# Two graph attention layers on sparse edges: three row tiles put first, their edges from five late tiles gathered apart, and light and heavy tiles interleaved

## The chip, the cores and the metric

The kernel runs on one core of one Trainium2 chip, in one launch, without help from the host. The metric is the device time in microseconds of a whole execution, as a median over several runs.

## The reference

There are 4096 nodes with 512 features and an adjacency matrix of 4096 x 4096 integers. An edge from node i to node j is likelier the smaller both numbers are, so the first row tiles have many edges and the last few. Two blocks follow one another, each with the old value added and a layer norm:

```
def attention(x, adj, W, a):                # for each head
    h = x @ W                               # 4096 x 64, eight heads (or x 512, one head)
    e = leaky_relu(src(h)[:, None] + dst(h)[None, :], 0.2)
    e = where(adj > 0, e, very_negative)
    return softmax(e, axis=-1) @ h

x = layernorm(x + attention(x, adj, W, a))              # block 0: 8 heads of 64
h = elu(attention(x, adj, W1, a1))                      # block 1: 8 heads of 64
h = elu(attention(h, adj, Wo, ao))                      #          1 head of 512
y = relu(h @ lin1_w + lin1_b) @ lin2_w + lin2_b         #          512 -> 1024 -> 512
x = layernorm(x + y)
```

A node without any edge gets the mean of all h, which is what the softmax over equal scores gives.

## The kernel before, in words

The kernel works on edges, not on the full matrix. Nodes stand in 32 row tiles of 128. There are four stages.

**Edge search** (find_edges). For each row tile, its part of the adjacency is loaded (raw), turned into signs by ScalarE (sg), and TensorE builds a key for each column (key); VectorE takes the largest eight of each segment and sorts them out into a list (cand, lst). ScalarE and GpSimd then find where each row's edges begin and end in one long list for the tile (degs, counts, starts, ends, sides), TensorE lays the list out (pl), and the result is idx: chunks of 128 edges each, one edge a partition, whose value is the number of the column's node. nl says to which row the edge belongs. A `Part` is such a list over a range of columns; tile 0 has four, every other tile one. There are 35 parts and 309 chunks: tile 0 has 51 chunks, tile 1 has 21, tiles 5 and 6 have 11, tiles 7, 9 and 10 have 10, 9 and 9, tiles 31 to 29 have 5. Beside it, the projection for layer 0 is made (`beside`).

**Layer 0 and layer 1** (heads_layer, called twice), and the **tail** with layer 2 and the two dense layers. Each layer has a table in DRAM with one row of projected values for each node and one more, row N, with their mean. A tile's chunks are cut into units of at most six chunks. For each unit:

- `gather` takes a buffer g and issues one indirect DMA on GpSimd's queue for each chunk, which brings 128 table rows;
- `spread` brings the rows' own scores to the edges with small matmuls (pss), once a tile;
- `weights` adds the gathered scores (z) and takes the exponent on ScalarE;
- `add` builds a selection matrix (sm), scales the gathered rows (g, line 1200; in layer 2 the weight goes into sm, line 1187), and TensorE accumulates them by row into acc (line 1212).

After a tile's last unit its sum is divided, normed and projected for the next layer's table: divide, norm, project, rows and split are steps that `run` takes one at a time between the units of the following tiles, so that a tile's row is written some units after its last accumulation. `rows` calls project_out, whose DMA on the SP queue writes 128 rows of the next table (line 711); `split` prepares the scores of eight tiles. Row N needs all tiles: mean_of_all_but makes it from all but the last tile ahead of the last unit, and finish_mean adds the last and writes it (line 770). In the layers the order of the tiles is 31 down to 0, in the tail it is written out by hand in `blocks` of two or four tiles, because the dense layers (first_dense, second_dense; 16 matmuls of 512 columns to a piece) work on a block at a time. Their pieces are spread over the units of the next block by `pace` and `due`.

Which instruction stands where on each engine's queue follows from this program order, since these stages run under a manual schedule; DMA issues on SP can be moved by the framework when what they wait for is ready earlier. Buffers set how far gathers run ahead:

```
g buffers in layers 0 and 1:  GB = 7, gather(units[i + GB]) stands right after add(units[i])
g buffers in the tail:        GT = 4, another pool, opened when the layers' pools are closed
order in each iteration:      weights(units[i + 1]); add(units[i]); gather(...); the ways of earlier tiles
```

In layer 0 ScalarE clears the seven buffers first (line 1286), in the tail GpSimd clears the four (line 1424). The tail then loads the weights of the dense layers on SP (lines 1428 to 1434) and turns the first bias with a transpose on TensorE (line 1503).

Of the kernel before, what the change touches and what calls it, by code (L numbers as in the profile page):

```python
# [10 lines left out]
F32 = mybir.dt.float32  # L11
# [29 lines left out]
GC = 6  # L41
GB = 7
KW = 512
FAR = -1e30
WIDE = 21
GT = 4

# [23 lines left out]
class Part:  # L71
# [5 lines left out]
    def __init__(self, t, lo, hi, last):  # L77
        self.t, self.lo, self.hi, self.last = t, lo, hi, last
        top = t * P
        r = 3 if t == 0 else 1  # L80
        self.segs = []
        j = lo
        while j < hi:
            lim = min(hi, (j // 1024 + 1) * 1024)
            lam, k = 0.0, j
            while k < lim:
                more = lam + rate(top, k)
                if k - j >= 8 * r and tail(more, 8 * r) > 3e-7:
# [20 lines left out]
        assert self.off > 0 and self.chunks[0] + self.chunks[1] >= self.n  # L109

# [448 lines left out]
def sparse_path(  # L559
# [291 lines left out]
    def find_edges(big, sb, ps, pk, constants, sg, beside):  # L851
# [12 lines left out]
        for v, p in enumerate(pts):  # L864
            t, k, c0, nch = p.t, p.k, p.first, p.n
            if t > 0:
                sg = signs_of(sb, t)
# [151 lines left out]
    def blocks_in(p, lo, m):  # L1019


        out = []
        for i in range(p.blocks):
            mine = [(g, c - lo) for g, c in enumerate((i, p.off + i)) if i < p.chunks[g] and lo <= c < lo + m]
            if len(mine) == 2:
                out.append((i, slice(0, 2), slice(mine[0][1], mine[1][1] + 1, p.off)))
            elif mine:
                g, c = mine[0]
                out.append((i, slice(g, g + 1), slice(c, c + 1)))
        return out  # L1030

    class Unit:

        def __init__(self, t, runs, slots):
            self.t, self.runs, self.slots = t, runs, slots
            self.chunks = [c for first, n in runs for c in range(first, first + n)]
# [10 lines left out]
    def units_of(order):  # L1049
        units = []  # L1050
        for t in order:
            own = [
                Unit(t, [(p.first + i, n) for i, n in runs], slots)
                for p in pts if p.t == t for runs, *slots in p.units()
            ]
# [9 lines left out]
    class Attention:  # L1065
# [6 lines left out]
        def gather(self, u):  # L1072

            u.g = self.gp.tile([P, GC, F + HS], F32, name="g")
            for k, c in enumerate(u.chunks):
                nc.gpsimd.indirect_dma_start(  # L1076
                    out=u.g[:, k, : self.st.row],
                    out_offset=None,
                    in_=self.st.table[:, :],
                    in_offset=bass.IndirectOffsetOnAxis(ap=idx[:, c : c + 1], axis=0),  # L1080
                    bounds_check=N,
                    oob_is_err=False,
# [187 lines left out]
    def heads_layer(gp, wk, sb, pp, st, nxt, fetch, finish, clear):  # L1270

        order = list(range(NT - 1, -1, -1))
        units = units_of(order)
        with tc.tile_pool(name=f"ha_{st.name}", bufs=2, space=PSUM, reuse_waits="tile") as pacc, \
# [5 lines left out]
            if clear:  # L1283
                for _ in range(GB):
                    g = gp.tile([P, GC * (F + HS)], F32, name="g")
                    nc.scalar.activation(g, ones.to_broadcast(g.shape), AF.Copy, scale=0.0)
            for u in units[:GB]:
                at.gather(u)
            for t in order[:2]:
# [23 lines left out]
            def split(t):  # L1313
                split_s(pp, nxt, t, 8)

# [7 lines left out]

            ways = []
            for i, u in enumerate(units):
# [16 lines left out]
                if u.first and pos > 0:  # L1342
                    ways.append((divide, order[pos - 1]))
                    run(divide)
                if spread:
                    spread()
            ways.append((divide, order[-1]))
            while ways:
# [57 lines left out]
    layers.close()  # L1406
    with tc.tile_pool(name="tg", bufs=GT, side="right", reuse_waits="tile") as gp, \
            tc.tile_pool(name="tb", bufs=1, side="right", reuse_waits="tile") as big, \
# [5 lines left out]
        few = NT - 12  # L1414
        blocks = [[NT - 1, NT - 2], [NT - 3 - i for i in range(NJ)]]
        blocks += [[1 + b, few // 2 - b, few // 2 + 1 + b, few - b] for b in range(few // NJ)]
        blocks.insert(3, [NT - 9, 0, NT - 8, NT - 7])
        blocks.append([NT - 10, NT - 11])
# [3 lines left out]
        at = Attention(st2, gp, wk, pacc, ps)  # L1422
        for _ in range(GT):
            nc.gpsimd.memset(gp.tile([P, GC, F + HS], F32, name="g"), 0.0)
        for u in units[:GT]:
            at.gather(u)
        l1w = big.tile([P, FC, HID], F32, name="sl1w")
# [84 lines left out]
        for i, u in enumerate(units):  # L1512
# [9 lines left out]
            at.add(u)  # L1522
            if i + GT < len(units):
                at.gather(units[i + GT])
            close()
# [71 lines left out]
```

## Time and profile before

| | us |
|---|---|
| median of 3 runs | 2143.87 (2143.78 to 2149.99) |
| the profiled execution | 2328.89 |
| its span, first to last instruction | 2326.7 |
| edge search | 0 to 497 |
| layer 0 (first gather to first gather) | 500 to 1032 |
| layer 1 | 1032 to 1556 |
| tail | 1556 to 2327 |

| engine | busy us | share of the span |
|---|---|---|
| PE (TensorE matmul) | 1776.6 | 76% |
| DVE (VectorE) | 1328.1 | 57% |
| POOL (GpSimd) | 1161.8 | 50% |
| ACT (ScalarE) | 658.9 | 28% |

In the page, PEld is TensorE's loading of weights, SP the queue of the direct DMAs, and L1212 is line 1212 of the kernel. A line of a timeline has the start, the duration, the engine, the line, the operation, what it writes and reads, the number of instructions merged, and in brackets the idle time before it with what ended it. The busy time of POOL counts a gather's descriptor work, not the transfer. The granted TensorE clock was 0.885 of full speed on average.

### The profile page before, as it was taken

How to read it: one execution, taken by the hardware profiler on the slowest of the kernel's cores; microseconds unless marked ns; L12 is line 12 of the kernel's file. 1: busy time of each engine (PE TensorE's matmuls, PEld its weight loads, DVE VectorE, ACT ScalarE, POOL GpSimd, SP SyncE). 2: the span in 40 equal slices, each digit the busy share in tenths (PEclk: the TensorE clock that was granted, in tenths of full speed). 3: DMA queues.
4: the chain of work that ended last, by engine and by line, in shares of the span. 5: the costliest groups of instructions: out<-in, count | busy, mean ns of one | idle time of the engine just before them, and what ended most of it. 6: DMA issues, size and time to landing. Idle time of an engine off the chain costs nothing.

```text
span 2326.7 us, 29282 instructions
## 1 busy us (share of the span) xinstructions
PE 1776.6 (76%) x8987; PEld 1038.4 (45%) x8987; DVE 1328.1 (57%) x3920; ACT 658.9 (28%) x2311; POOL 1161.8 (50%) x1662
## 2 busy tenths in 40 slices
PE   4778776643987775754997767746999898998997
PEld 3555442212665543531665444424445444444444
DVE  6887776744998776733777655733243424334322
ACT  3446776650332211100433221101111111121121
POOL 5424444456556664627556665646355634444300
PEclk9989997866999896875999988877999999999999
DMA  6434665525667775625566665545354524335301
GB/s 222 141 115 159 224 256 207 210 80 163 201 209 219 212 209 144 174 60 145 154 159 170 175 182 145 158 128 143 87 150 131 170 81 148 101 110 151 93 16 52
DMA packets 132589, 351.94 MB, mean 151 GB/s; under 512 B 41922, under 2 KB 42954, under 8 KB 128454
## 3 DMA queue, kind: packets, MB, share of 16 engines
q0 software_dynamic: 74160, 206.25, 33.1%
q1 hardware_dynamic: 58262, 143.72, 17.5%
q8 instruction: 74, 1.21, 0.2%
q14 instruction: 93, 0.76, 0.1%
HBM read 347.31 MB, written 42.24 MB: 167 GB/s over the span
## 4 chain that ended last, share of the span: by engine, by line
PE 36%; DVE 12%; issue 9%; another core or an unknown queue 6%; DMA 3%; POOL 3%; ACT 2%; SPq 0%; DVEq 0%; POOLq 0%; ACTq 0%
PE acc L1212 13%; PE p L1475 9%; PE ph L697 6%; PE p L1487 5%; DVE g L1200 4%; POOL g L1076 3%; DMA g<-table_t,idx 2%; DMA xr<-sx_d 1%; PE pt L683 1%; DVE bs L1253 1%; DVE sm L1179 1%; DVE sm L1187 1%; DVE xr L1492 1%; DVE z L1147 1%
## 5 line engine op out<-in xcount | busy, mean ns | idle before, releaser
L1076 POOL DMA_INDIRECT g<-table_t,idx x927 | 937.4, 1011 | 720.1 <-PE acc L1212 352.9
L1212 PE MATMUL acc<-g,sm 128*64 128x260 f32 (+2 forms) x4068 | 619.9, 424 | 219.9 <-DVE g L1200 100.7
L1212 PEld LDWEIGHTS acc<-g,sm 128*64 128x64 f32 x4068 | 347.9, 150 | 462.7 <-issue 177.8
L697 PE MATMUL ph<-sw_t,xt 128*128 128x264 f32 (+1 forms) x1536 | 408.4, 415 | 82.1 <-ACT xt L686 46.3
L697 PEld LDWEIGHTS ph<-sw_t,xt 128*128 128x128 f32 x1536 | 303.4, 204 | 154.2 <-ACT xt L686 63.0
L1200 DVE TENSOR_TENSOR g<-g,wp 128x2048 f32<-128x2048 f32 (+3 forms) x132 | 349.1, 2645 | 22.8 <-ACT wp L1155 20.2
L884 DVE MAX8 cand<-key 128x8 f32<-128x353 f32 (+55 forms) x467 | 197.3, 449 | 77.7 <-PE key L878 77.1
L1475 PE MATMUL p<-sht,sl1w 128*128 128x512 f32 (+1 forms) x576 | 229.3, 553 | 2.2 <-issue 1.2
L1487 PE MATMUL p<-sl2w,shid 128*128 128x512 f32 x512 | 227.0, 598 | 0.0
L686 ACT ACTIVATE xt<-pt 128x128 f32<-128x128 f32 x384 | 101.1, 278 | 286.5 <-PE pt L683 132.3
L710 ACT COPY hrow<-ph 128x260 f32<-128x260 f32 (+2 forms) x194 | 71.1, 373 | 311.1 <-PE ph L697 146.2
L1475 PEld LDWEIGHTS p<-sht,sl1w 128*128 128x128 f32 x576 | 107.6, 191 | 114.0 <-issue 108.7
L1487 PEld LDWEIGHTS p<-sl2w,shid 128*128 128x128 f32 x512 | 95.4, 190 | 120.1 <-issue 119.3
L1249 DVE SCALAR_TENSOR_TENSOR o<-ex,o 128x512 f32<-128x512 f32 x64 | 44.4, 694 | 182.8 <-ACT ex L1248 145.1
L877 PE MATMUL key<-sg,s_identb 128*128 128x512 bf16 (+1 forms) x258 | 111.6, 434 | 15.4 <-DVE cand L884 10.1
L848 ACT ACTIVATE sg<-raw 128x4096 bf16<-128x4096 int32 (+1 forms) x39 | 116.9, 2998 | 6.6 <-DMA raw<-in_adj_dram 3.7
L1478 ACT ACTIVATE shid<-p,sl1b 128x512 f32<-128x512 f32 (+1 forms) x72 | 46.0, 639 | 249.5 <-PE p L1475 212.0
L878 PE MATMUL key<-frac,places 128*128 128x512 bf16 (+1 forms) x258 | 111.1, 431 | 2.7 <-POOL places L784 2.7
L1187 DVE TENSOR_SCALAR sm<-iota_n,nl,w 128x64 f32<-128x64 f32 x339 | 83.1, 328 | 31.9 <-ACT w L1158 31.1
L1147 DVE TENSOR_TENSOR z<-s,g 128x16 f32<-128x16 f32 (+9 forms) x291 | 43.6, 174 | 92.0 <-DMA g<-table_t,idx 83.7
L1117 DVE TENSOR_REDUCE s<-pss 128x48 f32<-128x144 f32 (+21 forms) x108 | 32.1, 298 | 102.3 <-remote 55.1
L686 ACT ACTIVATION_READ_ACCUMULATOR xt<-pt 128x1 f32 x384 | 79.7, 208 | 0.0
(185 smaller groups left out, 1811.3 us busy)
## 6 DMA issues: line engine op xcount, KB each, us to landing
raw<-in_adj_dram SPq DMA_DIRECT2D x31, 2048.0 KB
table_t<-hrow SPq DMA_DIRECT2D x64, 260.0 KB
xr<-in_x_dram SPq DMA_DIRECT2D x64, 256.0 KB
g<-table_t,idx POOLq DMA_INDIRECT x927
table_t<-hrow SPq DMA_DIRECT2D x32, 257.0 KB
sx_d<-o SPq DMA_DIRECT2D x32, 256.0 KB
xr<-sx_d SPq DMA_DIRECT2D x32, 256.0 KB
out_dram<-xr SPq DMA_DIRECT2D x32, 256.0 KB
```

Of the source, the lines that this page charges most:

```text
L686: nc.scalar.activation(xt[:, c, :], pt[:, c, :], AF.Copy, accum_out=st.xparts[:, c, t : t + 1])
L697: nc.tensor.matmul(ph[:n], columns(c), st.w[:, c, j], start=(c == 0), stop=(c == FC - 1))
L848: nc.scalar.activation(sg[:, ts(i, w)], raw[:, ts(i, w)], AF.Sign)
L877: nc.tensor.matmul(out_, ident_b, sg[:, j:e], start=True, stop=False)
L878: nc.tensor.matmul(out_, places[:, w], frac[:, j - w * KW : e - w * KW], start=False, stop=True)
L884: nc.vector.max(out=cand[:, at : at + 8], in_=part)
L1076: nc.gpsimd.indirect_dma_start(out=u.g[:, k, : self.st.row], out_offset=None, in_=self.st.table[:, :], in_offset=bass.IndirectOffsetOnAxis ...
L1187: nc.vector.tensor_scalar(sm[:, at + i], of_g, node[k], u.w[:, k], op0=OP.is_equal, op1=OP.mult)
L1200: nc.vector.tensor_mul(body, body, wp[:, :, :, None].to_broadcast(body.shape))
L1212: nc.tensor.matmul(out_[g * HN : (g + 1) * HN], sm[:, slot], rows(k), start=start, stop=stop)
L1475: nc.tensor.matmul(p1, l1w[:, c, ts(k, P)], hts[b][:, c, :n], start=(c == 0), stop=(c == FC - 1))
L1487: nc.tensor.matmul(p2, hids[b][:, k, ts(j, P)], l2w[:, k, :], start=(k == 0), stop=(k == HC - 1))
```

## The change

Three tiles, 7, 9 and 10, are put first in every layer (FIRST). The part of each of them is cut in two at column 27 x 128 = 3456 (LATE): the edges to the nodes of tiles 0 to 26 and those to tiles 27 to 31. The late part comes to one chunk for each of the three; the number of all chunks stays 309, the parts become 38. The late chunks are units of their own with buffers of their own (pool "ll", GL = 3, one chunk each). A main unit of such a tile gathers from table rows below 3456 alone, so that it has no need of the last five tiles' rows or of row N.

The order in layers 0 and 1 (ORDER) is 7, 9, 10, then pairs of a tile with few edges and one with many (26, 5, 25, 13, 24, 4, 23, 12, 22, 0, 21, 11, 20, 1, 19, 6, 18, 2, 17, 8, 16, 3), then 15, 14 and 27 to 31. The tail's blocks are [7, 9], [10, 24, 25, 26], [20 to 23], [31, 0, 30, 29], [1, 14, 15, 16], [2, 17, 18, 6], [3, 5, 19, 11], [4, 8, 12, 13], [27, 28].

A class Gathering issues the gathers. It takes the units in order as long as a buffer of their kind is free; at the start of layer 1 and of the tail it puts the late units of FIRST behind as many main units of FIRST as there are buffers (six in layer 1, which is all of them; three in the tail). GB becomes 6, GT becomes 3. Three of the six buffers lie in a pool that stays through the tail ("lk"), so the tail has no memsets. The mean is made once 31 tiles have been projected, and split is called when all eight tiles of a group are there.

```diff
-GB = 7
+GB = 6
+GL = 3
+FIRST = [7, 9, 10]
+LATE = 27 * P
+MANY = [5, 13, 4, 12, 0, 11, 1, 6, 2, 8, 3]
+ORDER = FIRST + [t for pair in zip(range(26, 15, -1), MANY) for t in pair] + [15, 14] + list(range(27, NT))
-GT = 4
+GT = 3
...
-    return out + [Part(t, 0, N, True) for t in range(1, NT)]
+    for t in range(1, NT):
+        out += [Part(t, 0, LATE, False), Part(t, LATE, N, True)] if t in FIRST else [Part(t, 0, N, True)]
+    return out
...
+            self.late = p.lo == LATE
+            self.rows = N + 1 if p.last else p.hi
...
+    class Gathering:
+        def __init__(self, units, buffers, early=True):
+            ahead = []
+            for u in units:
+                if not early or u.t not in FIRST or sum(not v.late for v in ahead) == buffers:
+                    break
+                ahead.append(u)
+            ahead.sort(key=lambda u: u.late)
+            self.todo = ahead + [u for u in units if u not in ahead]
+            self.free = [buffers, GL]
+
+        def go(self, gather, done=None):
+            if done:
+                self.free[done.late] += 1
+            while self.todo and self.free[self.todo[0].late]:
+                u = self.todo.pop(0)
+                self.free[u.late] -= 1
+                gather(u)
...
-            u.g = self.gp.tile([P, GC, F + HS], F32, name="g")
+            u.g = small.tile([P, 1, F + HS], F32, name="gl") if u.late else self.gp()
-                    in_=self.st.table[:, :],
+                    in_=self.st.table[: u.rows, :],
-                    bounds_check=N,
+                    bounds_check=u.rows - 1,
...
-        order = list(range(NT - 1, -1, -1))
+        order = ORDER
-            for u in units[:GB]:
-                at.gather(u)
+            gathers = Gathering(units, GB, not clear)
+            gathers.go(at.gather)
...
-                return (split, t) if t % 8 == 0 else None
+                out_.add(t)
+                lo = t // 8 * 8
+                return (split, lo) if out_.issuperset(range(lo, lo + 8)) else None
...
-                if i == len(units) - 1:
-                    mrow = mean_of_all_but(pp, ps, nxt, u.t)
                 at.add(u)
-                if i + GB < len(units):
-                    at.gather(units[i + GB])
+                gathers.go(at.gather, u)
...
             while ways:
                 for of in (project, split, rows, norm, divide):
                     run(of)
+                    if mrow is None and len(out_) == NT - 1:
+                        mrow = mean_of_all_but(pp, ps, nxt, order[-1])
...
+    keep = ctx.enter_context(tc.tile_pool(name="lk", bufs=GT, reuse_waits="tile"))
+    small = ctx.enter_context(tc.tile_pool(name="ll", bufs=GL, reuse_waits="tile"))
-    gp = layers.enter_context(tc.tile_pool(name="lg", bufs=GB, side="right", reuse_waits="tile"))
+    more = layers.enter_context(tc.tile_pool(name="lg", bufs=GB - GT, side="right", reuse_waits="tile"))
+    def gp():
+        turns[0] += 1
+        return (keep if (turns[0] - 1) % GB < GT else more).tile([P, GC, F + HS], F32, name="g")
...
-        for _ in range(GT):
-            nc.gpsimd.memset(gp.tile([P, GC, F + HS], F32, name="g"), 0.0)
-        for u in units[:GT]:
-            at.gather(u)
+        gathers = Gathering(units, GT)
+        gathers.go(at.gather)
```

More of the change, by code (lines that the diff above doesn't have):

```diff
@@ L108, in __init__ @@
         self.off = self.n - self.chunks[1]
-        assert self.off > 0 and self.chunks[0] + self.chunks[1] >= self.n
+        assert self.chunks[0] + self.chunks[1] >= self.n
     def units(self):
@@ L865, in find_edges @@
             t, k, c0, nch = p.t, p.k, p.first, p.n
-            if t > 0:
+            if t > 0 and p.lo == 0:
                 sg = signs_of(sb, t)
@@ L1024, in blocks_in, with __init__ @@
             mine = [(g, c - lo) for g, c in enumerate((i, p.off + i)) if i < p.chunks[g] and lo <= c < lo + m]
-            if len(mine) == 2:
+            if len(mine) == 2 and p.off:
                 out.append((i, slice(0, 2), slice(mine[0][1], mine[1][1] + 1, p.off)))
-            elif mine:
-                g, c = mine[0]
-                out.append((i, slice(g, g + 1), slice(c, c + 1)))
+            else:
+                out += [(i, slice(g, g + 1), slice(c, c + 1)) for g, c in mine]
         return out
     class Unit:
-        def __init__(self, t, runs, slots):
-            self.t, self.runs, self.slots = t, runs, slots
+        def __init__(self, p, runs, slots):
+            self.t, self.runs, self.slots = p.t, runs, slots
+            self.late = p.lo == LATE
+            self.rows = N + 1 if p.last else p.hi
             self.chunks = [c for first, n in runs for c in range(first, first + n)]
@@ L1052, in units_of @@
             own = [
-                Unit(t, [(p.first + i, n) for i, n in runs], slots)
+                Unit(p, [(p.first + i, n) for i, n in runs], slots)
                 for p in pts if p.t == t for runs, *slots in p.units()
@@ L1283, in heads_layer @@
             if clear:
-                for _ in range(GB):
-                    g = gp.tile([P, GC * (F + HS)], F32, name="g")
-                    nc.scalar.activation(g, ones.to_broadcast(g.shape), AF.Copy, scale=0.0)
-            for u in units[:GB]:
-                at.gather(u)
+                for i in range(GB + GL):
+                    g = gp() if i < GB else small.tile([P, 1, F + HS], F32, name="gl")
+                    flat = g.rearrange("p k f -> p (k f)")
+                    nc.scalar.activation(flat, ones.to_broadcast(flat.shape), AF.Copy, scale=0.0)
+            gathers = Gathering(units, GB, not clear)
+            gathers.go(at.gather)
             for t in order[:2]:
@@ L1310, in rows, with split @@
                 project_out(pp, nxt, halves, t)
-                return (split, t) if t % 8 == 0 else None
-            def split(t):
-                split_s(pp, nxt, t, 8)
+                out_.add(t)
+                lo = t // 8 * 8
+                return (split, lo) if out_.issuperset(range(lo, lo + 8)) else None
+            def split(lo):
+                split_s(pp, nxt, lo, 8)
             def run(of):
@@ L1322, in run @@
                             ways.append(nxt_)
-            ways = []
+            ways, out_ = [], set()
             for i, u in enumerate(units):
@@ L1342, in heads_layer @@
                 if u.first and pos > 0:
+                    assert units[i - 1].last
                     ways.append((divide, order[pos - 1]))
@@ L1347, in heads_layer @@
             ways.append((divide, order[-1]))
+            mrow = None
             while ways:
@@ L1384, in sparse_path @@
     pp = layers.enter_context(tc.tile_pool(name="lp", bufs=2, side="right", reuse_waits="tile"))
-    gp = layers.enter_context(tc.tile_pool(name="lg", bufs=GB, side="right", reuse_waits="tile"))
+    more = layers.enter_context(tc.tile_pool(name="lg", bufs=GB - GT, side="right", reuse_waits="tile"))
+    turns = [0]
+    def gp():
+        turns[0] += 1
+        return (keep if (turns[0] - 1) % GB < GT else more).tile([P, GC, F + HS], F32, name="g")
     def fetch0(t):
@@ L1406, in sparse_path @@
     layers.close()
-    with tc.tile_pool(name="tg", bufs=GT, side="right", reuse_waits="tile") as gp, \
-            tc.tile_pool(name="tb", bufs=1, side="right", reuse_waits="tile") as big, \
+    with tc.tile_pool(name="tb", bufs=1, side="right", reuse_waits="tile") as big, \
             tc.tile_pool(name="ta", bufs=2, space=PSUM, reuse_waits="tile") as pacc, \
             tc.tile_pool(name="tp", bufs=1, space=PSUM, reuse_waits="tile") as ps, tc.manual_schedule():
[L1414 to L1418, printed above, removed]
+        blocks = [FIRST[:2], [FIRST[2], 24, 25, 26], [20, 21, 22, 23], [31, 0, 30, 29]]
+        blocks += [[1, 14, 15, 16], [2, 17, 18, 6], [3, 5, 19, 11], [4, 8, 12, 13], [27, 28]]
         assert sorted(sum(blocks, [])) == list(range(NT))
@@ L1421, in sparse_path @@
         units = units_of(order)
-        at = Attention(st2, gp, wk, pacc, ps)
-        for _ in range(GT):
-            nc.gpsimd.memset(gp.tile([P, GC, F + HS], F32, name="g"), 0.0)
-        for u in units[:GT]:
-            at.gather(u)
+        at = Attention(st2, lambda: keep.tile([P, GC, F + HS], F32, name="g"), wk, pacc, ps)
+        gathers = Gathering(units, GT)
+        gathers.go(at.gather)
         l1w = big.tile([P, FC, HID], F32, name="sl1w")
@@ L1522, in sparse_path @@
             at.add(u)
-            if i + GT < len(units):
-                at.gather(units[i + GT])
+            gathers.go(at.gather, u)
             close()
```

## The prediction

> **What bounds the kernel now.** I read the busy time by stage first, then the POOL and PE timelines at the two changes of layer, then the waits. In the windows the columns after the stretch are its length and the busy time of PE, PE's weight load, DVE, ACT and POOL, then the granted clock.
>
> ```profile
> 0.00:497.00 497.00, 348.54 (x1736) 200.69 (x1737) 370.82 (x1415) 292.18 (x842) 213.40 (x730) 0.89 0.51 179
> 497.00:1031.00 534.00, 374.47 (x2238) 245.05 (x2237) 373.50 (x842) 117.53 (x589) 312.54 (x311) 0.84 0.61 178
> 1031.00:1556.00 525.00, 374.49 (x2235) 243.18 (x2235) 313.52 (x648) 121.63 (x583) 323.03 (x313) 0.85 0.58 157
> 1556.00:2327.00 771.00, 679.11 (x2778) 349.51 (x2778) 270.27 (x1016) 127.56 (x298) 312.81 (x310) 0.94 0.39 111
> ```
>
> These are the edge search, layer 0, layer 1 and the tail. No engine fills the two layers, but a gather occupies POOL longer than its busy time says: successive ones start 1.30 us apart (1.00 busy, 0.30 issue). A layer has 309 chunks, so 309 x 1.30 = 402 us is its floor on POOL, and a layer takes 532 and 525 from first gather to first gather. The tail is PE's (679 of 771).
>
> At the first change of layer, POOL, then PE:
>
> ```profile
> 1031.74 1.00 POOL L1076 DMA_INDIRECT g<-table_t,idx  x1 [39.65 <-DMA table_t<-mrow]
> ...
> 1027.56 1.04 PE L768 MATMUL ph<-hrow,s_share 128*1 128x260 f32 x4 [0.53 <-ACT ss_t L717]
> 1051.17 5.29 PE L1212 MATMUL acc<-g,sm 128*64 128x260 f32 x24 [22.57 <-DVE g L1200]
> ```
>
> POOL is idle until the mean's row is in the table; PE waits until the first chunks are gathered and scaled. The last accumulation of layer 0 ended at 1014.8, so the next layer's first starts 36 us after it. At the second change, POOL, PE and SP:
>
> ```profile
> 1551.01 5.34 POOL L1424 MEMSET g<- 128x3120 f32 x2 [2.69 <-DMA table_t<-mrow]
> 1556.51 1.00 POOL L1076 DMA_INDIRECT g<-table_t,idx  x1 [0.16 <-POOL g L1424]
> ...
> 1551.40 0.27 PE L1503 MATMUL pt<-s_ident,sl1b_r 8*128 8x8 f32 x1 [1.36 <-DMA sl1b_r<-in_lin_b_dram]
> 1572.90 5.85 PE L1212 MATMUL acc<-g,sm 128*64 128x257 f32 x24 [21.02 <-DMA g<-table_t,idx]
> ...
> 1525.04 0.38 SPq L1428 DMA_DIRECT2D sl1w<-in_lin_w_dram  x1
> 1526.79 0.38 SPq L1430 DMA_DIRECT2D sl2w<-in_lin_w_dram  x1
> 1549.68 0.25 SPq L770 DMA_DIRECT2D table_t<-mrow  x1
> 1549.99 0.30 SPq L1432 DMA_DIRECT2D sl1b_r<-in_lin_b_dram  x1
> ```
>
> Last accumulation 1534.8, first of the tail 38 us later. Note SP: the two weight loads go out 25 us before the mean's row. Last, from the chain of waits around the first change:
>
> ```profile
> 1065.71 36.79 another core or an unknown queue
> ```
>
> There PE takes about 1.4 us a matmul with its operands ready. Such pieces recur (20.3 us at 860, 13.6 at 1378) and name no engine.
>
> The profiled execution took 2328.9 us (span 2326.7), 185 more than the median of 2143.87. I assume that these unnamed stalls are most of the 185, so I work with steps free of them and carry the difference in us to the median.
>
> **The Trainium skill.** "DMA: Bandwidth & Descriptors", Queues, rings and completion order: on each DMA engine descriptors are taken in ring order, and SP owns one row of rings. No run shows it yet; it matters in part 5. "Runtime: NRT & Kernel Launch", Instruction fetch mechanics: each sequencer streams its instructions by a DMA queue of its own, a cost "mostly hidden". The trace agrees that such queues run (two instruction queues, 167 packets) and cannot say whether they cause the stalls. "TensorE: Matmul & The Clock Gate", Part 1: after an idle window PE runs at half clock; here the clock reads 0.50 from 1555 to 1575 and 24 matmuls take 5.85 us against 3.48 in the next unit.
>
> **The change, part by part.**
>
> 1. Edge search: three more parts. Each adds on ACT about ten small operations: 0.31 + 0.30 + 0.19 on the list, 0.26 + 0.25 + 0.26 on the counts, two 128-wide sides at some 0.4 (0.61 for 384 wide), 0.52, 0.15: 3.0 us; on POOL 13 operations, some 3.5 us; on DVE about 1.3. In the built program the next tile's adjacency sign (3.6 us) stands behind them on ACT. A tile's period at 245 to 257 is 11.7 us with 3.6 of ACT idle, so 3.0 each could hide in part, or a wait for the counts (1.9) comes on top. **+12 (4 to 20).**
> 2. Start of layer 0: the clearing of buffers, 18.95 us of ACT for seven, holds the first exponent until 514.6. Six large and three small are 16.3 + 1.4. **-1.** Ahead of the first accumulation nothing else changes: 28 chunks are fetched early where 42 were, and only the first two units' matter to it.
> 3. Order within layers. Periods between tiles in layer 0 are 8.6 us for 6 chunks (DVE has no gap; POOL needs 7.8), 10 for 7 and 13 for 9 (POOL 9.1, 11.7), and POOL's own 14.3 for 11 chunks. Summed without stalls the old order gives some 434, less up to 30 that seven buffers carry from light to heavy tiles: 405 to 434 against the floor of 402. So alternating can win little, and six buffers in place of seven couple the engines tighter. **-4 a layer, -8 (-25 to +12).** The nine added one-chunk units (three a layer) cost DVE some 1.7 us each, and tiles 7 and 9 get three more accumulation slots of 0.46; beside POOL most of it hides. **+3 (0 to 8).**
> 4. Change to layer 1. The early gathers read rows 0 to 3455; in the built program the first of them waits for fewer table writes than the late ones, so they do pass the last five tiles. The six buffers come free as tile 14's second unit and tiles 27 to 31 end; 25 gathers are 33 us, and at 8.6 us a tile they start some 13 us before the last accumulation. The drain grows: two projections (3.7 each) and the mean's (3.7) that the old order did beside tile 0 now follow the last accumulation; some of it fills gaps, so finish_mean ends 19 us after it, not 14. From there to the first matmul is 5.5 (scores 1.5, z 0.65, exponent 0.4, sm 0.5, scaling 2.3): 24.5 against 36.4, 12 us. Then the old kernel is fed at 6.5 us a unit while DVE needs 3.9, 13 us over five units; the new one has 28 chunks in place. Counted on POOL: its 29th gather goes out at +26 (first buffer free) against 17 + 28 x 1.30 = +53. **-23 (-27 to -12).**
> 5. Change to the tail. Only three buffers outlive the layers, so 13 chunks and one late one are early. The four memsets go; two of them (5.3 us) lay ahead of the first gather. But in the built program SP now has both weight loads behind the mean's row, since their memory is that of the last tiles' buffers, and the small sl1b_r behind them; PE's transpose of sl1b_r stands ahead of the first accumulation. The loads are 4.2 MB; the 249, 395 and 197 GB/s of the three 5 us stretches from 1525 say 12.3 us. With drain +5 (mean's row +20, sl1b_r issued +21) PE goes on at +35 against +38. What is then gathered lets the dense pieces start at some +53, against +60 in the old kernel freed of stalls (72 as profiled). **-7 (-20 to +5).**
> 6. The tail with three buffers for four. weights(i+3) stands on DVE ahead of the scaling of unit i+2, and waits for a gather that starts when unit i is done: 7.8 us for 6 chunks plus 3.1 to 3.7 to land (the chain's gather waits), 11 us, to be covered by two units. 66 units over 750 us are 11 each, so the mean covers it; in tile 0's block of 66 chunks eight dense pieces of 7 us lie between sixteen units of 2.8, and pairs without a piece don't. **+6 (0 to 20).**
>
> Sum: 12 - 1 - 8 + 3 - 23 - 7 + 6 = **-18**: 2311 profiled, 2143.9 - 18 = **2126** as median.
>
> **The rivals.**
> - Slower: the third tail buffer decides. If a pair of units without a dense piece (5.5 us) meets the 11 us gather some six times, 6 x 5.5 = 33 us come in place of the 6, and with reordering at its upper half (+3, not -8) the sum is +20: **2164**. For it: POOL's waits on acc (231 us in the tail) say that buffers, not POOL, time the gathers. Against: DVE waited only 24 us for gathers in the tail with four. It decides from two units shorter than 11 us in a row.
> - Both changes of layer pay in full and the mixing reaches the POOL floor: -1 - 25 + 3 - 27 - 20 + 6 + 6 (edge search half hidden) = -58: **2086**. For it: 40 us of POOL idle. Against: POOL must then never wait in a layer where DVE alone has 374 us of work.
> - The early gathers wait for the whole table after all: then 4 and 5 turn into the longer drain (+5 each), and 12 - 1 - 8 + 3 + 10 + 6 = +22: **2166**. The built program's waits speak against it.
>
> **How the numbers follow.** About 0.3%, 6.4 us, is what a measurement of this kernel can tell from no change. Forecast 0.50 (of it 0.42 beyond -6.4, 0.08 within), full gain 0.13, third buffer 0.27 (0.04 within), early gathers blocked 0.05, something unnamed on the slow side 0.05. That gives faster 0.55, same 0.12, slower 0.33. The ends of all parts add to -75 and +57; they won't meet at once, so the range takes in both named rivals and stops at 2082 and 2178.
>
> **What would show it.** Right: gathers of table 1 on POOL before the mean's row, PE's gap at the first change (22.6 us) under 10; at the second change a PE wait for sl1b_r of some 12 us; the edge search 8 to 16 us longer. Wrong: DVE z or PE acc waiting for gathers in the tail by far more than 24 us, an edge search longer by over 25, or layers longer from first gather to first gather though the changes of layer are short.

## The result, and the profile after

| | before | after |
|---|---|---|
| median of 20 runs each, us | 2142.44 (2138.20 to 2149.99) | 2138.46 (2132.75 to 2144.04) |
| ratio | | 0.9984 (95% interval 0.9976 to 0.9992) |
| the profiled execution, its span | 2139.84, 2137.5 (b_again, below) | 2138.82, 2137.1 |

The change wins 4.0 us (0.2%) where 18 were forecast. The execution of the kernel before that the prediction reads held 185 us of stalls, 84 and 82 of them in the two layers, that its timed runs don't have; so the kernel after is set here against a second profile of the kernel before, b_again, which is free of them.

The windows by stage, with the columns of the prediction (length, busy PE, PE's weight load, DVE, ACT, POOL, granted clock, DMA share, GB/s). They are cut at the first gather and at the DMAs of the two mean rows, since gathers now cross the changes of layer. The kernel before:

```profile
0.00:498.60 498.60, 348.68 (x1740) 200.49 (x1740) 371.15 (x1416) 294.80 (x843) 213.58 (x731) 0.89 0.51 180
498.60:944.10 445.50, 348.38 (x2234) 229.53 (x2234) 370.94 (x840) 116.37 (x588) 312.45 (x309) 0.91 0.71 211
944.10:1381.30 437.20, 342.31 (x2226) 228.53 (x2227) 313.08 (x645) 123.37 (x583) 318.36 (x311) 0.91 0.69 188
1381.30:2137.50 756.20, 672.89 (x2787) 345.30 (x2786) 270.72 (x1020) 127.80 (x298) 320.07 (x311) 0.95 0.40 114
```

The kernel after:

```profile
0.00:504.40 504.40, 355.82 (x1770) 207.82 (x1771) 374.02 (x1434) 299.88 (x876) 221.87 (x799) 0.87 0.51 178
504.40:963.60 459.20, 358.45 (x2277) 233.95 (x2276) 379.88 (x876) 118.14 (x600) 339.06 (x334) 0.90 0.74 216
963.60:1385.80 422.20, 344.51 (x2221) 227.04 (x2218) 308.63 (x650) 123.63 (x585) 299.74 (x297) 0.93 0.67 179
1385.80:2137.10 751.30, 674.19 (x2804) 344.91 (x2803) 274.09 (x1035) 128.50 (x301) 299.48 (x296) 0.95 0.40 116
```

Edge search +5.8 us, layer 0 +13.7, layer 1 -15.0, tail -4.9: -0.4 in all. POOL's count says what crossed: the stretch of layer 0 holds 334 gathers in place of 309, and the 25 more are the early ones of layer 1. The stretch is longer all the same; why, the experiments have to show.

The first change of layer, on POOL, SP, PE and DVE, in the kernel after (start, duration, engine, line, operation, and in brackets the idle time before it):

```profile
912.43 0.99 POOL L1111 DMA_INDIRECT g<-table_t,idx  x1 [0.30 <-issue]
929.78 1.09 POOL L1111 DMA_INDIRECT g<-table_t,idx  x1 [16.36 <-PE ph L708]
...
966.26 1.00 POOL L1111 DMA_INDIRECT gl<-table_t,idx  x1 [3.30 <-DMA table_t<-mrow]
...
924.92 0.42 SPq L722 DMA_DIRECT2D table_t<-hrow  x1
...
963.57 0.24 SPq L781 DMA_DIRECT2D table_t<-mrow  x1
...
960.83 0.66 PE L1247 MATMUL acc<-g,sm 128*64 128x260 f32 x4
...
969.45 0.17 DVE L1182 TENSOR_TENSOR z<-s,gl 128x8 f32<-128x8 f32 x1 [5.91 <-DMA gl<-table_t,idx]
...
973.34 5.46 PE L1247 MATMUL acc<-g,sm 128*64 128x260 f32 x24 [9.42 <-DVE g L1235]
```

and in the kernel before (b_again):

```profile
911.50 1.00 POOL L1076 DMA_INDIRECT g<-table_t,idx  x1 [0.30 <-issue]
946.07 1.00 POOL L1076 DMA_INDIRECT g<-table_t,idx  x1 [33.58 <-DMA table_t<-mrow]
...
965.59 4.97 PE L1212 MATMUL acc<-g,sm 128*64 128x260 f32 x24 [22.65 <-DVE g L1200]
```

The early gathers run as forecast: table 1 is read from 929.8, 34 us ahead of the mean's row (issued at 963.6), and PE's largest gap falls from 22.7 to 9.4 us. They don't start when POOL is free (913.4) but 16.4 us later. The profile names PE for that wait; by the program it is for the last row below 3456, that of tile 14, whose write goes out at 924.9 (the median time to landing of these writes is 3.6 us).

PE begins layer 1 earlier than the 973.3 that the expectation of a_noearly below reckons from: the first unit of tile 7 is accumulated from 960.8, before the mean's row goes out. What then holds PE is the late chunk. Its scores stand on DVE ahead of the scaling of tile 7's second unit, and DVE waits 5.9 us for its gather, which had to wait for the mean's row.

The second change in the kernel after, POOL, SP and PE:

```profile
1388.02 0.99 POOL L1111 DMA_INDIRECT gl<-table_t,idx  x1 [20.73 <-DVE z L1183]
1406.40 0.99 POOL L1111 DMA_INDIRECT g<-table_t,idx  x1 [17.38 <-PE acc L1247]
...
1386.77 0.38 SPq L1468 DMA_DIRECT2D sl1w<-in_lin_w_dram  x1
1387.34 0.38 SPq L1470 DMA_DIRECT2D sl2w<-in_lin_w_dram  x1
1387.78 3.24 SPq L1472 DMA_DIRECT2D sl1b_r<-in_lin_b_dram  x1
...
1400.87 0.27 PE L1543 MATMUL pt<-s_ident,sl1b_r 8*128 8x8 f32 x1 [13.70 <-DMA sl1b_r<-in_lin_b_dram]
1402.64 5.87 PE L1247 MATMUL acc<-g,sm 128*64 128x257 f32 x39 [0.79 <-DVE sm L1222]
```

Thirteen chunks are in place, but PE stands for 13.7 us at the transpose of the bias, whose load was issued behind 4.2 MB of weights, and POOL, whose buffers wait for PE, stands 17.4 us more. The first gather of the tail starts 37 us earlier than before (1350.7 against 1388.1), its first accumulation 2 us earlier (1402.6 against 1404.5), its first dense piece 5 us later (1435.2 against 1430.5).

### The profile page after: what moved, and what is told of

Read it like the earlier page. It is cut to its first block, busy times and chain, and to the rows that moved or that the text cites. A ratio compares the mean times of both kernels' runs of the same rounds, so it can differ in the third digit from the quotient of the medians.

```text
span 2137.1 us, 29672 instructions
## 1 busy us (share of the span) xinstructions
PE 1733.0 (81%) x9067; PEld 1013.7 (47%) x9067; DVE 1336.6 (63%) x3994; ACT 670.1 (31%) x2361; POOL 1160.1 (54%) x1725
## 4 chain that ended last, share of the span: by engine, by line
PE 37%; issue 16%; DVE 14%; POOL 14%; DMA 12%; ACT 6%; SPq 0%; POOLq 0%; DVEq 0%; ACTq 0%
PE acc L1247 11%; DMA g<-table_t,idx 10%; POOL g L1111 9%; PE ph L708 8%; PE p L1515 7%; PE p L1527 6%; DVE g L1235 3%; ACT sg L859 1%; DVE cand L895 1%; POOL s L955 1%; PE pt L694 1%; DMA xr<-sx_d 1%; DVE cand L912 1%; PE key L888 1%; PE key L889 1%
## 5 line engine op out<-in xcount | busy, mean ns | idle before, releaser
L1247 PE MATMUL acc<-g,sm 128*64 128x260 f32 (+2 forms) x4032 | 586.4, 422 | 169.3 <-DVE g L1235 138.1
L1247 PEld LDWEIGHTS acc<-g,sm 128*64 128x64 f32 x4032 | 329.3, 149 | 389.6 <-DVE g L1235 158.8
L708 PE MATMUL ph<-sw_t,xt 128*128 128x264 f32 (+1 forms) x1536 | 396.6, 406 | 56.4 <-ACT xt L697 49.9
L1235 DVE TENSOR_TENSOR g<-g,wp 128x2048 f32<-128x2048 f32 (+3 forms) x132 | 345.8, 2620 | 16.9 <-ACT wp L1190 16.8
L708 PEld LDWEIGHTS ph<-sw_t,xt 128*128 128x128 f32 x1536 | 293.7, 198 | 127.4 <-ACT xt L697 72.9
L895 DVE MAX8 cand<-key 128x8 f32<-128x8 f32 (+57 forms) x469 | 195.9, 445 | 77.3 <-PE key L889 76.4
L888 PE MATMUL key<-sg,s_identb 128*128 128x512 bf16 (+3 forms) x261 | 113.2, 436 | 13.7 <-DVE cand L895 8.6
L889 PE MATMUL key<-frac,places 128*128 128x512 bf16 (+3 forms) x261 | 113.3, 435 | 2.6 <-POOL places L795 2.6
L1190 ACT ACTIVATE wp<-z 128x32 f32<-128x32 f32 (+3 forms) x138 | 28.3, 205 | 193.1 <-DVE g L1235 188.6
```

What stands on the lines that cost most here:

```text
L708: nc.tensor.matmul(ph[:n], columns(c), st.w[:, c, j], start=(c == 0), stop=(c == FC - 1))
L888: nc.tensor.matmul(out_, ident_b, sg[:, j:e], start=True, stop=False)
L889: nc.tensor.matmul(out_, places[:, w], frac[:, j - w * KW : e - w * KW], start=False, stop=True)
L895: nc.vector.max(out=cand[:, at : at + 8], in_=part)
L1235: nc.vector.tensor_mul(body, body, wp[:, :, :, None].to_broadcast(body.shape))
L1247: nc.tensor.matmul(out_[g * HN : (g + 1) * HN], sm[:, slot], rows(k), start=start, stop=stop)
```

## The experiments

Three accounts of the 14 us that are missing from the forecast stand against each other. Theory A: three buffers in the tail, one fewer than before, took back what the changes of layer won. B: the edge search and the late units did. C: the order within the layers did. Each run was timed beside the kernel before; a difference to the kernel after is the difference of the two distances from the kernel before.

**b_again**, the kernel before once more. 

> The kernel before once more, for a profile without the unnamed stalls. If the stalls of the first profile were the 185 us, this one has a span near 2140 us; layer 0 and layer 1 from first gather to first gather then come to some 460 and 455 us (532 and 525 were profiled), the tail to some 730 us, DVE's waits for gathers stay under 90 us in all. If the stalls belong to the kernel, the span is again some 2300 us.

 It took 2139.84, span 2137.5, with layers of 447 and 442 us from first gather to first gather. The kernel can run without the stalls. The tail, from its first gather on, takes 749 us where 730 were expected, and DVE's waits for gathers come to 154 us in the whole run, not to less than 90.

**b_gt3**

```diff
-GT = 4
+GT = 3
```

> The kernel before with three gather buffers in the tail in place of four, nothing else. Theory A (the tail's third buffer takes back what the changes of layer gained): slower by 15 to 30 us, about 2160, and DVE z waits for gathers in the tail for 80 us or more. Rival B (the gain is lost in edge search and late units) and rival C (lost in the order within the layers): within 5 us of the kernel before.

 2163.4 against 2141.1, ratio 1.0104 (1.0087 to 1.0121): +22 us, all in the tail (21.4 longer from layer 1's last division). DVE's waits for gathers in the tail rise from 53.8 to 157.3 us. A's mechanism holds: a buffer less costs that much.

**b_parts**, the kernel before with

```diff
...
+        out += [Part(t, 0, LATE, False), Part(t, LATE, N, True)] if t in FIRST else [Part(t, 0, N, True)]
...
```

> The kernel before with the parts of tiles 7, 9 and 10 cut in two at column 3456; order, buffers and early fetching as before. Theory A and rival C: slower by 8 to 12 us (an edge search some 5 us longer, three more one-chunk units a layer). Rival B: slower by 20 us or more, with most of it in the edge search.

 2183.7, ratio 1.0198 (1.0182 to 1.0215): +43 us. The first gather is 6.4 us later, layer 0 is 22.7 longer to its last division, layer 1 1.0, the tail 13.7. So B is wrong in its place: most is not in the edge search. What it is in layer 0 shows on POOL alone, in the stretch that holds layer 0's 309 gathers (length, busy POOL, granted clock, DMA share, GB/s), first in the kernel before, then in b_parts:

```profile
498.00:912.60 414.60, 312.45 (x309) 0.91 0.77 226
```

```profile
505.00:940.30 435.30, 312.83 (x309) 0.89 0.74 215
```

309 gathers at 1.30 us are 402; the kernel before takes 413 from its first to its last with 9 us of idle POOL beyond the 0.3 us between two issues, b_parts 434 with 32. Of the 32, 23 lie between 705 and 758, where the tiles about the three cut ones pass, and all but one of the six idle spells there end with an accumulation, which frees a buffer. A one-chunk unit in one of the seven shared buffers shortens the run-ahead by up to five chunks; that this is the cause is argued, not isolated, and layer 1 hardly shows it. In the kernel after the late units have buffers of their own.

**a_bias**, the kernel after with

```diff
+    lb = ctx.enter_context(tc.tile_pool(name="lb", bufs=1, reuse_waits="tile"))
+    l1b_r = lb.tile([HC, P], F32, name="sl1b_r")
+    nc.sync.dma_start(l1b_r, lin1_b.rearrange("(c p) -> c p", p=P))
...
-        l1b_r = big.tile([HC, P], F32, name="sl1b_r")
-        nc.sync.dma_start(l1b_r, lin1_b.rearrange("(c p) -> c p", p=P))
```

> The kernel after, with the first bias loaded to a buffer of its own before the layers, so that TensorE's transpose of it at the second change of layer has nothing to wait for. If that wait of 13.7 us is on the path: 10 to 13 us faster than the kernel after, about 2127. If something else is late there (the late gathers behind the mean's row, the first dense weights): 0 to 4 us faster, and the gap at 1387 stays under another name.

 2124.4, ratio 0.9922 (0.9907 to 0.9936): set against the kernel before in each comparison (-16.7 and -4.0 us) it is 13 us faster than the kernel after. PE at the second change:

```profile
1390.06 3.54 PE L1247 MATMUL acc<-g,sm 128*64 128x257 f32 x16 [0.48 <-DVE sm L1222]
```

From the mean's row to the first accumulation it is 3.3 us where it was 16.8: within the noise the whole wait was on the path.

**a_merge**, the kernel after with each late chunk in the buffer of its tile's second main unit (nine units fewer):

```diff
...
+            if t in FIRST:
+                main, late = own[:-1], own[-1]
+                own = main[::-1]
+                own[-1].join(late)
...
```

> The kernel after without units of one chunk: the late chunk of tiles 7, 9 and 10 goes, by a gather of its own, into the buffer of the tile's second main unit, which then has five chunks. Theory D (a unit costs a round of the chain from VectorE over ScalarE to TensorE, some 4 to 7 us, however few chunks it has): nine rounds less, 15 to 30 us faster than the kernel after, about 2115, and layer 0 shorter by some 8 us. Rival (a late unit costs its own 1.7 us of VectorE and hides else): 0 to 6 us faster, about 2134.

 2155.6, ratio 1.0059 (1.0044 to 1.0075): 16 us slower than the kernel after, against both expectations. No layer is shorter (to the last division 439.5 against 440.3, then 426.4 against 423.6): with buffers of their own the late units cost next to nothing, and theory D falls. Why it is slower is only partly located. Its profile is 10.9 us longer than that of the kernel after: 4.3 before the first gather, 2.0 in the layers, 4.5 in the tail, where the stretch from first accumulation to first dense piece takes 43.8 us for 32.6.

**a_plain**, the kernel after without alternation:

```diff
-ORDER = FIRST + [t for pair in zip(range(26, 15, -1), MANY) for t in pair] + [15, 14] + list(range(27, NT))
+ORDER = FIRST + [t for t in range(26, -1, -1) if t not in FIRST] + list(range(27, NT))
```

> The kernel after with 7, 9, 10, then the other tiles from 26 down to 0, then 27 to 31 in the two layers: no alternation of few and many edges. If alternating is worth what I forecast (4 us a layer): 5 to 12 us slower than the kernel after. Rival 1 (alternating costs, since six buffers can't carry light tiles over heavy ones any better): 5 to 15 us faster. Rival 2 (the alternation holds the layers together): 25 us slower or more.

 2158.0, ratio 1.0068 (1.0052 to 1.0084): 19 us slower than the kernel after, between the first expectation and rival 2. POOL idles 20 and 21 us inside the layers' gathers, 2 and 8 in the kernel after. So with 7, 9 and 10 in front, light tiles at the end and six buffers, the alternation is needed. That does not make it better than the old descending order: with six buffers that one takes 435.4 us for layer 0 (n_gb6, below), less than the 440.3 of the kernel after.

**b_blocks** and **b_blk3**, the kernel before with the tail's blocks of the kernel after, b_blk3 with GT = 3 as well:

```diff
-        blocks = [[NT - 1, NT - 2], [NT - 3 - i for i in range(NJ)]]
...
+        blocks = [[7, 9], [10, 24, 25, 26], [20, 21, 22, 23], [31, 0, 30, 29]]
...
```

> The kernel before with the blocks of the tail in the order of the kernel after (7 and 9 first), four buffers as before, nothing else. Theory A: the order of blocks by itself moves the time by less than 6 us. Rival: the new order pays by itself, 8 to 15 us faster, since tile 0 stands among tiles without dense work waiting.

 

> The kernel before with the blocks of the tail in the order of the kernel after and three buffers in the tail. Theory A (the third buffer costs in the new order what it costs in the old one): 15 to 28 us slower than the kernel before, 2157 to 2170. Rival (the new order covers the three buffers): within 8 us of the kernel before.

 b_blocks 2129.0, ratio 0.9937 (0.9920 to 0.9954): the order pays 14 us by itself, as the rival said. b_blk3 2146.3, ratio 1.0014 (1.0006 to 1.0021): again as the rival said, the new order covers the three buffers. In the new order the missing buffer costs 17 us, in the old one 22. DVE's waits for gathers in the tail (us, times, longest), in b_again, after, b_blocks and b_blk3:

```profile
DVE z L1147 <- DMA g<-table_t,idx: 53.8, 15, 15.1
```

```profile
DVE z L1182 <- DMA g<-table_t,idx: 128.6, 37, 7.6
```

```profile
DVE z L1147 <- DMA g<-table_t,idx: 68.5, 17, 11.0
```

```profile
DVE z L1147 <- DMA g<-table_t,idx: 150.5, 42, 8.4
```

Three buffers in place of four add 82 us of such waits in the new order and 104 in the old one (b_gt3), of which about a fifth comes through to the end. That the rest falls in times in which PE has dense pieces is likely, but no run shows it.

**a_best4, a_noearly, b_gb6, b_order.** In this series every kernel ran with the stalls of the first profile (the kernel before took 2320.9), so the four were measured again, as n_best4, n_noearly, n_gb6 and n_order, against 2143.3. Edits: a fourth buffer in the tail of a_bias, two of the late buffers ending with the layers to make room; no early gathers (`self.rows = N + 1`, and `early` off); GB = 6 in the kernel before; the new ORDER, with mean and split as in the kernel after, in the kernel before.

> The kernel after with a fourth gather buffer in the tail again (the memory comes from two of the three late buffers, which now end with the layers) and the first bias loaded before the layers. If the price of the third buffer (17 us, from 2129.0 to 2146.3 in the new order) and that of the bias (14 us) add up: 2138 - 17 - 14 = 2107 (2102 to 2112). Rival: the two are one wait, since both let the tail's first gathers go earlier: 2120 to 2125, as with the bias alone.

 

> The kernel after with nothing fetched across the changes of layer: the main units of 7, 9 and 10 are gathered from the whole table, so they wait for row N like all others. Theory: the early gathers are worth what the first change showed, some 12 us of TensorE's gap (9.8 against 21.5 from the mean's row to the first accumulation) and some 8 us of feeding after it; at the second change the bias stands in their way: 20 to 30 us slower than the kernel after, about 2163. Rival (only the gap counts): 10 to 14 us slower. Rival 2 (the gap is refilled later by gathers that run ahead): under 6 us slower.

 

> The kernel before with six gather buffers in the layers in place of seven. Theory: the sixth and seventh buffer carry light tiles over heavy ones in the descending order, which is why layer 0 of the kernel after took 9 us more to its last division: 8 to 16 us slower than the kernel before, both layers longer. Rival (the layers got longer for other reasons, tiles 7, 9 and 10 in front): within 4 us of the kernel before.

 

> The kernel before with the new order in the two layers alone (7, 9, 10 in front, then few and many in turn, 14, 15 and 27 to 31 last), whole parts, seven buffers, no early fetching, the tail as before. Theory: alternating wins 10 us a layer against the descending order, the longer drain takes 5 back: 5 to 15 us faster than the kernel before. Rival: with seven buffers the descending order is as good, the drain remains: 5 to 12 us slower.

There the ratios were 1.0067 (1.0043 to 1.0091), 1.0136 (1.0112 to 1.0159), 0.9955 (0.9936 to 0.9974) and 1.0227 (1.0199 to 1.0254).

> The kernel after with a fourth gather buffer in the tail and the first bias loaded before the layers, as in a_best4. If both prices add up: 2138 - 17 - 14 = 2107 (2102 to 2112), ratio to before some 0.984. Rival: they are one wait: 2120 to 2125, ratio 0.991.

 2117.4, ratio 0.9886 (0.9869 to 0.9904), between the two. Against the kernel before it wins 25.9 us where the bias alone won 16.7: the fourth buffer adds 9, not 17. DVE's waits for gathers fall all the same:

```profile
DVE z L1182 <- DMA g<-table_t,idx: 47.4, 14, 7.9
```

From the mean's row to 2110 us PE is then busy for 673 of 724 us (658 in the kernel after): 51 us of idle PE are left there. It is the best version that ran, ahead of both kernels.

> The kernel after with nothing fetched across the changes of layer, as in a_noearly. Theory: 20 to 30 us slower than the kernel after, about 2163 (ratio to before 1.01). Rival (only TensorE's gap at the first change counts): 10 to 14 us slower, about 2150. Rival 2 (later gathers refill it): under 6 us slower.

 2173.1, ratio 1.0147 (1.0126 to 1.0169): early gathers are worth some 34 us, more than the theory said. From last division to last division layer 1 takes 451.3 against 423.6 with them, 27.7; the tail is 4.2 longer.

> The kernel before with six gather buffers in the layers in place of seven, as in b_gb6. On the other chip it was 9 us faster than the kernel before, with both layers 5 us shorter, which speaks for the rival. Theory (the seventh buffer is worth some 8 us a layer): 8 to 16 us slower, about 2155. Rival (seven are no better than six): within 4 us of the kernel before.

 2154.7, ratio 1.0048 (1.0030 to 1.0066): +11 us, the layers 4.4 and 5.3 longer, the tail 4.2. The theory holds for the descending order; that the tail, which the edit doesn't touch, is longer too stays unexplained. In the new order the buffer makes no difference to layer 0: 440.3 us to the last division both with seven (n_order, next) and with six (the kernel after).

> The kernel before with the new order in the two layers alone, as in b_order. Theory E: the order in itself costs; 7, 9 and 10 in front have no light tiles ahead of them that would let gathers run ahead, and the drain is 4.5 us longer at each change: 15 to 35 us slower than the kernel before, about 2168, layer 0 longer by 10 or more from first gather to last division. Rival: alternating wins more than the drain costs: 5 to 15 us faster.

 2171.9, ratio 1.0139 (1.0118 to 1.0160): +29 us, with seven buffers and whole parts. So E, which is C made definite, holds: in the balance it is the order that explains the lost gain, since A's cost is covered by the new blocks and B's is 6 us. Layer 0 of n_order, its last gather, the divisions of its last five tiles and the first gather of layer 1 (POOL, DVE, POOL):

```profile
907.19 1.00 POOL L1079 DMA_INDIRECT g<-table_t,idx  x1 [0.31 <-issue]
...
910.76 0.20 DVE L1223 RECIPROCAL rd<-acc 128x8 f32<-128x8 f32 x1
918.67 0.20 DVE L1223 RECIPROCAL rd<-acc 128x8 f32<-128x8 f32 x1
928.00 0.20 DVE L1223 RECIPROCAL rd<-acc 128x8 f32<-128x8 f32 x1
934.86 0.20 DVE L1223 RECIPROCAL rd<-acc 128x8 f32<-128x8 f32 x1
941.63 0.20 DVE L1223 RECIPROCAL rd<-acc 128x8 f32<-128x8 f32 x1
...
962.54 1.00 POOL L1079 DMA_INDIRECT g<-table_t,idx  x1 [54.35 <-DMA table_t<-mrow]
```

and the last division of layer 0 in b_again, whose last gather started at 911.50:

```profile
929.68 0.21 DVE L1220 RECIPROCAL rd<-acc 128x8 f32<-128x8 f32 x1 [6.38 <-PE acc L1212]
```

The gathers of n_order are 7 us tighter (405.9 from first to last, with no idle POOL beyond the time between issues, against 412.9), but the last division follows the last gather by 34.4 us, not 18.2. The engines in these two stretches (columns as in the stages above), n_order first, then b_again:

```profile
907.19:941.63 34.44, 30.30 (x181) 20.71 (x182) 30.41 (x67) 9.88 (x58) 1.00 (x1) 0.90 0.30 103
```

```profile
911.50:929.68 18.18, 16.54 (x99) 9.10 (x100) 11.60 (x22) 1.80 (x7) 0.99 (x1) 1.00 0.04 11
```

In n_order five tiles are still to be accumulated and divided, 6.8 to 9.3 us apart, and DVE is busy for 30 of the 34 us; in b_again what is left belongs to one tile. In layer 1 of n_order the gathers are as tight as before (406.3 against 405.9), and the last division follows the last gather by 24.3 us, not 15.7.

**c_heavy3, c_heavy0**, n_best4 with another order in layer 1 alone:

```diff
+ORDER1 = FIRST + list(range(NT - 1, 26, -1)) + [15, 14] + [t for pair in zip(range(26, 15, -1), MANY) for t in pair]
...
-        order = ORDER
+        order = ORDER if clear else ORDER1
```

> n_best4 with another order in layer 1 alone: 7, 9, 10, then the light tiles 31 to 27, 15, 14, then the pairs of few and many, so that the layer ends with tile 3. If the end of the order is what costs (the last gather lies 24 us before the last division with light tiles last, 16 with heavy ones): layer 1 shorter by some 8 us, its drain by up to 4; the tail's early gathers then wait for tile 3's row, which gives 4 to 6 back: 2109 to 2114. Rival (the front costs: 7, 9 and 10 without light tiles ahead): 2117 to 2122, layer 1 as long as before.

 

> As c_heavy3, with tiles 0 and 3 exchanged, so that layer 1 ends with tile 0 and its 51 chunks. End theory: as c_heavy3 or up to 5 us better, since a heavy tile at the end has no light units left in the buffers: 2106 to 2114. Rival (the front costs): 2117 to 2122.

 2130.3, ratio 0.9949 (0.9930 to 0.9969), and 2123.6, ratio 0.9909 (0.9893 to 0.9925): slower than n_best4 and outside both expectations. In both the end is shorter: the last division follows the last gather by 13.4 us in c_heavy0 and 19.1 in c_heavy3, for 24.4 in n_best4. Layer 1 is 5.2 us shorter in c_heavy0 (412.8 for 418.0), but not in c_heavy3 (419.6), as the rival of the front has it; in both the gathers take 5 to 6 us more from first to last. So the pair bears out the end only in part. The whole is slower since the tail's early gathers need the row of the heavy tile that now comes last: none of them runs ahead of the mean's row, and the first accumulation comes 19.7 us (c_heavy0) and 20.0 us (c_heavy3) after it, not 3.3.

## Why the prediction was right or wrong

In the table a layer runs from last division to last division (layer 0 from its first gather). What lies between a layer's last division and the issue of the mean's row, the drain, falls to the next stage.

| step | forecast | measured | from |
|---|---|---|---|
| 1 edge search | +12 | +6 | first gather 498.6 to 504.4; 504.2 to 510.3 in the other kernels with cut parts |
| 2 start | -1 | -2 | first gather to first accumulation 19.7 to 17.6; part of the next line |
| 3 order, buffers, late units | -5 | +18.3 | layer 0 +9.2 (431.04 to 440.26); layer 1 of n_order 451.6 - 437.9 - 4.5 of drain = +9.1 |
| 4 first change | -23 | -23.2 | early gathers -27.7 (n_noearly), drain 14.4 to 18.9 |
| 5 second change | -7 | -4.4 | tail of b_blk3 773.3, of the kernel after 768.9 |
| 6 third buffer | +6 | +19.7 | tail of b_blocks 753.6, of b_blk3 773.3 |
| order of the blocks | no line | -16.3 | tail of b_again 769.9, of b_blocks 753.6 |

Layer 1 is 437.9 before and 423.6 after, -14.3, and the tail 769.9 and 768.9; 5.7 + 9.2 - 14.3 - 1.0 = -0.4, as between the spans.

**The step that failed is 3.** It priced the order by POOL's floor and by the periods between tiles, 405 to 434 us for the old order against 402, and let alternation win 4 us a layer of that; what a layer still has to do after its last gather had no term. On POOL there was little to win: the old order's gathers took 413 and 406 us from first to last, with 9 us of idle POOL in layer 0 and none in layer 1. The rest of a layer's length is the time from the last gather to the last division, and that is what the new order makes longer. n_order, with whole parts and seven buffers, shows the whole +9 of layer 0, so it is the order, not the cut parts or the sixth buffer. Its gathers did win 7 us in layer 0, and nothing in layer 1; the ends cost 16 and 9. The size stands clear of what else moves: layer 0 takes 430.8 to 431.0 us in b_again, b_gt3, b_blocks and b_blk3, and 438.2 to 442.3 in all eight kernels with the new order in layer 0 and without the stalls. The reason for the longer end, light tiles that still fill the buffers ahead of DVE when POOL has finished, where tile 0 leaves parts of one tile, fits the engines' times in n_order and c_heavy0. It is not the whole: c_heavy3 shortened the end and not the layer, so what the front of the order does in layer 1 stays open.

**Step 4 was right in its sum and in its main mechanism**: the reads pass the last rows, and the drain is 4.5 us longer (5 were forecast). How the sum comes about is other than forecast. From the last division to the next layer's first accumulation it is 16.2 us for 35.9, not 24.5 for 36.4, as the first unit needs nothing of the mean's row; then DVE's wait for the late chunk gives part of that back. Step 1 was half of its value, in the lower part of its range: each part added 1.9 us, not 4.

**Steps 5 and 6 were right only in their sum, and that by luck.** Step 5 won 4 us of its 7. Its wait for the bias was forecast at 12 us and measured at 13.7. The Trainium skill, "DMA: Bandwidth & Descriptors", Queues, rings and completion order, has descriptors taken in ring order; the 13.1 us from sl1b_r's issue to PE's transpose, against 1.4 in the kernel before, where it stood behind the mean's row alone, agree, and the second weight load, issued 0.4 us before it, took 13.8 to land. Step 6 was forecast at +6 and is +17 to +22 by the timed runs; it spread the gathers over the tail, 11 us a unit on average, and so allowed few waits, where DVE's waits came to over 80 us more. That units without a dense piece come in runs would explain it, but no run shows it unit by unit. And a term was missing: the new order of the blocks, which I gave no line, pays 14 us with four buffers and 19 with three. The rival of the third buffer, 33 us and slower, named the right sign, waits of DVE far above 24 us, and the measured cost lies about halfway between it and my 6; in the whole change the blocks' order covered it.

Two smaller errors: the ends of all parts add to -69 and +52, not to -75 and +57. And the sign "layers longer from first gather to first gather" could not show: with early gathers that stretch is 425.4 us for layer 0 against 447.4, although from first gather to last division layer 0 takes 9 us more.

**My assumption on the 185 us was right**: a profile without them exists, and nine tenths of them lie in the layers (515 and 520 us there, 431 and 438 in b_again, from first gather or last division to last division). Of the chain of work that ended last, the unnamed pieces are 5.9% in the first profile and none in b_again; in b_gb6, which has stalls of this size too, they are 1.9%, so the name alone doesn't find the stalls. What causes the stalls stays open; the record gives chip 8 both for the series with them and for the one without, whatever the expectation of n_gb6 says of another chip. In n_gb6 and b_gb6, the same kernel without and with them, PE's accumulation either runs on or stops between single matmuls:

```profile
552.38 2.85 PE L1212 MATMUL acc<-g,sm 128*64 128x260 f32 x24 [0.20 <-DVE g L1200]
```

```profile
549.02 0.59 PE L1212 MATMUL acc<-g,sm 128*64 128x260 f32 x1 [1.52 <-issue]
551.12 0.59 PE L1212 MATMUL acc<-g,sm 128*64 128x260 f32 x1 [1.50 <-issue]
```

That the instruction queues are behind it was not tried. Also open is why the new order of blocks pays: the largest wait of PE that shrinks in the tail is that of pt on DVE's o, 28.9 to 12.3 us (to 13.1 with three buffers), which no run isolates.

## What to carry to other kernels

Cut a layer at the engine that feeds it: the first-to-last time of its gathers against count times pace says how much an order can win, and the time from the last gather to the last division what it can lose. Work that is fetched across a barrier pays only as far as nothing else stands at that barrier; look at every small DMA that lands behind large ones there. When a change trades buffers for order, price each alone on both sides: here -14, +17, -34 and +29 us, with smaller ones, came out as -4.

## What the runs showed of the hardware

The same program took 2143 us and, in one series of runs, 2321; in the profiles nine tenths of the difference lie in the two layers and 1 us in the edge search. Differences between kernels did not carry over: six buffers for seven is +0.48% in the one and -0.45% in the other.
